# Moving one more shared chunk of a mixture-of-experts layer behind the last branch of a graph transformer kernel

## The chip, the cores and the metric

The kernel runs on one core of a Trainium2 chip. The metric is the device time of one execution in microseconds (us). The core has TensorE (PE, matmuls; its weight loads are shown apart as PEld), VectorE (DVE), ScalarE (ACT), GpSimd (POOL) and SyncE (SP), each with an instruction queue of its own that runs in order. Transfers are issued from SP (plain ones) and from POOL (indirect ones, with row numbers from a tile).

## The reference

The reference is a two-layer graph transformer over 3125 nodes with 256 features. Each layer adds a graph part, a mixing part and a feed-forward part to `x`. Only the feed-forward part of the second layer, a mixture of experts, is touched here:

```python
def _L1_ffn_ref(x, Wr, W1s, b1s, W2s, b2s, W1p, b1p, W2p, b2p):
    shared = gelu(x @ W1s + b1s) @ W2s + b2s          # every row; 256 -> 1024 -> 256
    rw = jax.nn.softmax(x @ Wr, axis=-1)              # 8 experts
    topw, topi = jax.lax.top_k(rw, K)                 # K = 2
    topw = topw / jnp.sum(topw, axis=-1, keepdims=True)
    mask = jnp.sum(jax.nn.one_hot(topi, E, dtype=topw.dtype) * topw[..., None], axis=-2)
    h = gelu(jnp.einsum('bsd,edf->bsef', x, W1p) + b1p)
    priv = jnp.einsum('bsef,efd->bsed', h, W2p) + b2p
    routed = jnp.einsum('bsed,bse->bsd', priv, mask)
    return shared + routed
```

Its input is the layer normalised `x`, and its result is added to `x`.

## The kernel before

The 3125 rows are 25 tiles of 125 rows. They are grouped in seven chunks (`CHUNKS`, line 23): chunks 0 to 5 hold four tiles (500 rows) and chunk 6 holds one (125 rows). The whole second layer is one function, `layer1`, with generators as its parts.

**The shared part** is `shared(c)` (line 1994). For a chunk it makes eight up groups (line 2012, tile `hp_s`: two matmuls each, `pw1s` against the turned rows `xT_f`), a gelu of each on ACT (line 2003, `hid_s`), and for each tile of 125 rows one down group of eight matmuls (line 2026, `dn_s`), whose result DVE adds to `X` (line 2029). A float32 matmul is recorded twice in the trace, so a chunk of 500 rows has 32 records on line 2012 and 64 on line 2026, 16 for each tile.

**The routed part** sorts the 6250 pairs of a row and an expert by expert. `scatter()` (lines 1975 to 1992) writes each row to its places in `xs` by 50 indirect transfers on POOL. The places are cut in `NT` = 32 tiles of 256 rows. `fetched(i)` (line 2032) fetches the expert's weights `rw` by two indirect transfers (line 2039), loads the rows `xr` on SP (line 2045) and turns them with PE (line 2056, `xrT`). The load waits for all 50 scatters. `routed(i)` (line 2065) is the two matmul layers with a gelu between them (line 2086, `rh`; line 2074; line 2101, `ry`), an addition of the bias on DVE (line 2108) and two indirect stores to `ys` on POOL (line 2111).

**The end.** `finish(t)` (line 2120) loads a tile's two routed results `yl` from `ys` (line 2123, two transfers each through `rows_dma`, line 208) and adds each with its gate to `X` on DVE (line 2126, two instructions a tile). The load comes after all stores (`stored_`). `collect(c)` (line 2130) stores a finished chunk to the output.

**The order of the work** is set by a planner, `Flow` (line 87), while the program is built. Each generator yields an `Op` with an engine, a cost in us, what it comes after, and buffers that it takes and gives back. `run` always issues the operation that can start earliest by these costs, and the lower urgency number where two start together. The engines then execute the instructions of each queue in that order. The buffers stand for real tiles: in this part PSUM has `mm` = 2, `nm` = 3 and `qe` = 2 banks (line 2223). `hp_s` takes `mm` and `qe` in turn, and both `ry` and `dn_s` take `nm`, which DVE's addition gives back. `shared` = 1 keeps two shared chunks from running at once. The eight `rhid` buffers hold the routed hidden rows and, at the end, the `yl` tiles.

The routed tiles that are always there and some of the shared chunks run in one long flow:

```python
            if c < LATE:
                flow.add(60 + c if c < 3 else 200 + c, shared(c))
...
            if i < NT - SPARE:
                flow.add(70 + i, routed(i))
```

The last `SPARE` = 2 routed tiles run in a branch, `tc.If(tiles > NT - SPARE)` (line 2181), which is taken only where the rows of the experts need more than 30 tiles. In the profiled execution it isn't taken (line 2086 has 960 records, 30 tiles of 32). Behind it a new flow with a clock of its own, the tail, holds the rest:

```python
        for c in range(LATE, len(CHUNKS)):
            shared_[c].time = None
        for c, (t0, nt) in enumerate(CHUNKS):
            if c >= LATE:
                flow.add(200 + c, shared(c))
            for t in range(t0, t0 + nt):
                flow.add(300 + c, finish(t))
            flow.add(300 + c, collect(c))
```

The costs that the planner has for the tail are: 0.0035 us a row for an up group (1.75 for 500 rows), 1.75 for four down matmuls, 0.42 for a shared addition, 0.6 with a lag of 3.5 for a `yl` load, 1.0 for a pair of routed additions, 0.1 for an output, and 0.2 between any two engines (`hop`). The planner takes all stores as done at time 0 of the tail.

Of the kernel before, what the change touches and what calls it, by code (L numbers as in the profile page):

```python
# [22 lines left out]
CHUNKS = [(t, min(4, T - t)) for t in range(0, T, 4)]  # L23
# [127 lines left out]
def kernel(ctx: ExitStack, tc: tile.TileContext, a: dict, out: bass.AP):  # L151
# [1311 lines left out]
    def layer1(lists):  # L1463
# [308 lines left out]


        RB = ROUTE // 128
        SPARE, LATE = 2, len(CHUNKS) - 2
        R = {"xT": [None] * len(CHUNKS)}
        logits_ = [Mark() for _ in CHUNKS]
        normal_ = [Mark() for _ in CHUNKS]
# [426 lines left out]
    def in_order():  # L2205
        with ExitStack() as st:
            psum(st, mm=4, nm=2, ed=2)
            first = Layer0(True)
            first.first()
            flow = Flow(mm=4, nm=2, ed=2, db=2, XT=5, qT=2, msg=2, S0=3, mlp=1, hT=1, hid=8,  # L2210
                        xh=2, xT=3, f_w=2, wT=1, ex=2, fh=3, qkv=2, q3=1)
            first.mixing_flow(flow)
            flow.add(-2, first.after_mixing())
            first.edges_flow(flow)
            first.mlp_flow(flow)
            flow.add(-2, first.after_mlp())
            first.soft_flow(flow)
            with tc.manual_schedule(engines=ENGINES):
                flow.run()
            for name in ("ffn", "fw", "e0"):  # L2220
                first.close(name)
        with ExitStack() as st:
            psum(st, mm=2, nm=3, qe=2, ed=1)
            layer1(True)

    def any_order():
# [40 lines left out]
        with ExitStack() as st:  # L2267
            psum(st, mm=2, nm=3, qe=2, ed=1)
            layer1(False)
# [104 lines left out]
```

## Time and profile before

| what | us |
|---|---|
| median of four runs | 2858.73 |
| lowest and highest of them | 2852.36, 2878.94 |
| the profiled execution | 2856.21 |
| its span in the trace | 2854.4 |
| PE busy in the span | 2513.8 (88%) |
| DVE, ACT, POOL busy | 1333.7, 975.3, 1180.6 |
| last scatter issued, first `xr` turned | 2339.98, 2355.59 |
| last routed matmul starts | within 2792.43 to 2796.05 |
| first `yl` load issued | 2807.07 |
| last addition starts | 2846.30 |

Times of the trace count from the start of its span. The page gives each engine's busy share in 40 slices, the chain of work that ended last, and the costliest groups of instructions by line. A row of a timeline has the start, the duration, the engine, the line, the operation with the names of its tiles, how many instructions are merged in the row, and in brackets how long the engine was idle before them and what ended that. A row of windows has a stretch, its length, the busy time of PE, PEld, DVE, ACT and POOL, the clock that TensorE was granted (1.00 is full), the DMA engines' share and GB/s.

### The profile page before, as it was taken

Reading aid. Unit: us, or ns where it says so; the run is one execution under the profiler, and the core shown is the slowest. Engines: PE = TensorE matmul, PEld = TensorE weight load, DVE = VectorE, ACT = ScalarE, POOL = GpSimd, SP = SyncE. Lnnn points to the kernel's source line nnn. Section 1 sums busy time; section 2 is a strip of 40 time slices with the busy share of each in tenths; the row PEclk is TensorE's granted clock in tenths of the full one; section 3 lists DMA queues with packets and bytes.
Section 4 is the critical chain, followed back from the end, with each engine's and each line's share of the span. In section 5 each row is a group of like instructions: output and inputs, shape, how many; then the busy total and the mean of one; then the engine's idle time right before and its main releaser. Section 6 shows DMA issues by size and latency. Waiting matters only on the chain. (4 is left out here: it accounts for less than half of the span.)

```text
span 2854.4 us, 31754 instructions
## 1 busy us (share of the span) xinstructions
PE 2513.8 (88%) x11281; PEld 1824.5 (64%) x11281; DVE 1333.7 (47%) x3223; ACT 975.3 (34%) x1997; POOL 1180.6 (41%) x1175
## 2 busy tenths in 40 slices
PE   3888898988899999996777888888888999999998
PEld 2545575655556555564555666666666768888886
DVE  5375113253343343445878687777788401111114
ACT  3673111221222333344334453444443212222221
POOL 3002676766674000002666566655562371222220
PEclk8989998999999999997889999989999999999999
DMA  4335556565564002506666556656550044555556
GB/s 107 127 103 168 156 152 187 156 172 170 153 201 111 26 15 75 130 22 209 209 189 202 172 186 195 180 161 193 183 173 31 19 133 149 194 194 194 194 194 192
DMA packets 186806, 426.48 MB, mean 149 GB/s; under 512 B 31370, under 2 KB 116490, under 8 KB 178443
## 3 DMA queue, kind: packets, MB, share of 16 engines
q0 software_dynamic: 80496, 281.25, 32.5%
q1 hardware_dynamic: 103593, 140.99, 15.8%
q10 hardware_dynamic: 2545, 2.09, 0.3%
q8 instruction: 92, 1.51, 0.2%
q14 instruction: 80, 0.65, 0.1%
HBM read 358.95 MB, written 65.22 MB: 149 GB/s over the span
## 5 line engine op out<-in xcount | busy, mean ns | idle before, releaser
L1083 POOL DMA_INDIRECT msg<-hs,el x425 | 418.0, 984 | 410.2 <-DMA hot<-S 210.5
L1524 POOL DMA_INDIRECT kvg<-kvtab,el x425 | 459.3, 1081 | 286.9 <-issue 116.7
L1195 ACT ACTIVATE fh<-fp,bnh,bns 128x500 f32<-128x500 f32 (+1 forms) x224 | 160.2, 723 | 406.8 <-PE fp L1191 291.6
L1601 PE MATMUL es<-kvg,S 128*125 128x264 f32 x850 | 226.9, 421 | 42.0 <-DVE kvg L1593 30.0
L1560 PE MATMUL qe<-q,ST 125*128 125x256 bf16 x1275 | 186.7, 291 | 65.1 <-DVE kvg L1564 41.9
L1206 DVE SCALAR_TENSOR_TENSOR x<-fy,f_w,x 125x256 f32<-125x256 f32 x200 | 95.8, 482 | 308.3 <-PE fy L1203 188.0
L1203 PE MATMUL fy<-f_Wo,fh 128*125 128x256 f32 x800 | 209.7, 386 | 29.5 <-DVE x L1206 17.3
L1601 PEld LDWEIGHTS es<-kvg,S 128*125 128x125 f32 x850 | 170.7, 206 | 89.9 <-DVE kvg L1593 39.3
L2086 PE MATMUL rh<-xrT,rw 128*128 128x256 f32 x960 | 223.7, 381 | 0.0
L2074 ACT ACTIVATE rhid<-rh,rw 128x256 f32<-128x256 f32 x240 | 113.7, 474 | 321.6 <-PE rh L2086 304.4
L1112 PEld LDWEIGHTS <-S 128*125 128x125 bf16 x1275 | 158.3, 142 | 96.3 <-issue 79.4
L2101 PE MATMUL ry<-rw,rhid 128*128 128x256 f32 x960 | 217.0, 379 | 0.0
L1112 PE MATMUL es<-msg,S 128*125 128x256 bf16 x1275 | 186.9, 283 | 27.6 <-DMA msg<-hs,el 14.7
L1560 PEld LDWEIGHTS <-ST 125*128 125x128 bf16 x1275 | 131.7, 103 | 110.5 <-issue 78.5
L2101 PEld LDWEIGHTS ry<-rw,rhid 128*128 128x128 f32 x960 | 182.4, 190 | 24.8
L1203 PEld LDWEIGHTS fy<-f_Wo,fh 128*125 128x125 f32 x800 | 142.8, 190 | 86.6 <-issue 33.4
L2086 PEld LDWEIGHTS rh<-xrT,rw 128*128 128x128 f32 x960 | 181.1, 191 | 24.1 <-issue 0.5
L1191 PE MATMUL fp<-fh,f_W 128*128 128x500 f32 (+1 forms) x448 | 187.8, 548 | 2.0 <-ACT fh L1195 2.0
L1191 PE MATMUL fp<-xT_f,f_W 128*128 128x500 f32 (+1 forms) x448 | 188.2, 548 | 0.0
L2108 DVE TENSOR_TENSOR yr<-ry,rw 128x256 f32<-128x256 f32 x60 | 25.5, 425 | 335.7 <-PE ry L2101 335.7
L1564 DVE TENSOR_TENSOR kvg<-qe,kvg 128x512 f32<-128x512 f32 (+1 forms) x225 | 144.6, 652 | 75.8 <-PE qe L1560 26.6
L1319 POOL TENSOR_TENSOR xn<-xn,row_bp 125x1024 f32<-125x1024 f32 (+1 forms) x7 | 13.8, 1975 | 386.7 <-DVE hx L1293 316.8
(426 smaller groups left out, 4246.2 us busy)
## 6 DMA issues: line engine op xcount, KB each, us to landing
db<-dlT SPq DMA_DIRECT2D x25, 544.0 KB
ST<-dlT SPq DMA_DIRECT2D x25, 544.0 KB
hot<-S SPq DMA_DIRECT2D x50, 187.5 KB
Sb<-hot SPq DMA_DIRECT2D x50, 187.5 KB
ztab<-z SPq DMA_DIRECT2D x18, 500.0 KB
z<-ztab SPq DMA_DIRECT2D x12, 750.0 KB
xs<-pad SPq DMA_DIRECT2D x1, 8224.0 KB
xr<-xs SPq DMA_DIRECT2D x32, 257.0 KB
```

The source lines that it names most:

```text
L1083: nc.gpsimd.indirect_dma_start(out=msg[:, i, :], out_offset=None, in_=hs3_rows, in_offset=bass.IndirectOffsetOnAxis(ap=el[:, b, g0 + i : g ...
L1112: nc.tensor.matmul(blk["po"], S[:, i, :], msg[:, i, r * C : (r + 1) * C], start=(g0 + i == 0 and r == 0), stop=(g0 + i == LE - 1 and r == 2))
L1191: nc.tensor.matmul(ps[q][:, :n], self.ws[e][i][:, k, q * 128 : (q + 1) * 128], h[:, k, :n], start=(k == 0), stop=(k == 1))
L1195: nc.scalar.activation(nxt[:, q, :n], ps[q][:, :n], AF.Relu, bias=self.sh[i][:, 2 * e + q : 2 * e + q + 1], scale=self.sc[i][:, 2 * e + q ...
L1203: nc.tensor.matmul(po, nxt[:, k, j * P : (j + 1) * P], self.ws[e][2][:, k, :], start=(k == 0), stop=(k == 1))
L1524: nc.gpsimd.indirect_dma_start(out=kvg[:, i, : 2 * C], out_offset=None, in_=kvtab, in_offset=bass.IndirectOffsetOnAxis(ap=el[:, b, g0 + i ...
L1560: nc.tensor.matmul(pq[i0][:, i, :], ST[:P, g0 + i0 + i, :], blk["q3"][:, r, :], start=(r == 0), stop=(r == 2))
L1564: nc.vector.tensor_tensor(kvg[:, i0 : i0 + k, :C], pq[i0][:, :k, :], kvg[:, i0 : i0 + k, :C], OP.mult)
L1601: nc.tensor.matmul(blk["pa"], S[:, i, :], kvg[:, i, C:], start=(g0 + i == 0), stop=(g0 + i == LE - 1))
L2074: nc.scalar.activation(hid[-1][:, q % 2, :], ps, AF.Gelu, bias=w1[:, 8 * C + q : 8 * C + q + 1])
L2086: nc.tensor.matmul(ps, w1[:, k * 4 * C + h * 128 : k * 4 * C + (h + 1) * 128], xrT[:, k, :], start=(k == 0), stop=(k == 1))
L2101: nc.tensor.matmul(po, hid[k // 2][:, k % 2, r * 128 : (r + 1) * 128], w2[:, k * C : (k + 1) * C], start=(k == 0), stop=(k == 7))
```

## The change

`LATE` is the number of the first shared chunk that runs in the tail. It was 5 and becomes 4.

```diff
         RB = ROUTE // 128
-        SPARE, LATE = 2, len(CHUNKS) - 2
+        SPARE, LATE = 2, len(CHUNKS) - 3
         R = {"xT": [None] * len(CHUNKS)}
```

`shared(4)` (32 records of line 2012, 8 gelus, 64 records of line 2026, 4 additions) is no longer a stream of the long flow. It becomes a stream of the tail, with the same urgency 204, ahead of `shared(5)` (205) and `shared(6)` (206). The tail then has three shared chunks, 500, 500 and 125 rows, beside the 25 loads and 25 pairs of additions. Nothing is computed that wasn't before, and no transfer is added or left out.

## The prediction

> **What bounds the kernel now.** I read the stage table of the page first: over the whole span PE is busy 88%, and from 2250 us on it shows 100% in nearly every slice. So I asked for the windows around the routed stage and the tail, in rows cut where the work changes.
>
> ```profile
> 2341.80:2352.00 10.20, 10.20 (x25) 4.37 (x23) 0.42 (x1) 3.39 (x5) 3.52 (x4) 1.00 0.88 310
> 2352.00:2355.50 3.50, 0.02 (x1) 0.00 (x0) 0.02 (x1) 0.00 (x0) 0.00 (x0) 0.79 1.01 415
> 2355.50:2364.00 8.50, 6.35 (x18) 4.78 (x19) 1.60 (x4) 1.52 (x3) 0.00 (x0) 0.50 0.38 120
> 2364.00:2796.00 432.00, 432.00 (x2053) 379.02 (x2052) 47.70 (x118) 113.71 (x240) 115.44 (x117) 1.00 0.54 188
> 2807.00:2820.50 13.50, 13.50 (x33) 6.16 (x34) 8.03 (x17) 4.74 (x7) 0.00 (x0) 1.00 0.90 206
> 2834.30:2841.50 7.20, 7.18 (x49) 6.38 (x47) 5.33 (x13) 2.94 (x8) 0.00 (x0) 1.00 0.90 269
> 2841.50:2854.40 12.90, 0.00 (x0) 0.00 (x0) 2.73 (x7) 0.00 (x0) 0.00 (x0) 0.66 0.44 125
> ```
>
> After the window and its length stand the busy us of PE, PEld, DVE, ACT and POOL, then the granted clock, DMA share and GB/s. The reader is to see three things: PE is the bound from 2364 to 2841.5 without a gap; just ahead of that it waits, at clock 0.50 when it resumes; and in the tail from 2807 the DMA (0.90) is as busy as PE, and the last 12.9 us hold no PE work.
>
> Then PE's timeline, to find where chunk 4 (16 up and 32 down matmuls, recorded as 32 and 64) runs today:
>
> ```profile
> 2341.80 10.22 PE L2012 MATMUL hp_s<-xT_f,pw1s 128*128 128x500 f32 x24
> 2355.59 1.09 PE L2056 MATMUL xrT<-ident,xr 128*128 128x128 f32 x4 [3.57 <-DMA xr<-xs]
> 2363.03 2.47 PE L2012 MATMUL hp_s<-xT_f,pw1s 128*128 128x500 f32 x4
> 2381.74 1.84 PE L2012 MATMUL hp_s<-xT_f,pw1s 128*128 128x500 f32 x4
> 2398.98 1.89 PE L2026 MATMUL dn_s<-pw2s,hid_s 128*125 128x256 f32 x8
> ...
> ```
>
> ```profile
> 2790.70 1.89 PE L2026 MATMUL dn_s<-pw2s,hid_s 128*125 128x256 f32 x8
> 2792.43 3.62 PE L2101 MATMUL ry<-rw,rhid 128*128 128x256 f32 x16
> 2795.88 1.89 PE L2026 MATMUL dn_s<-pw2s,hid_s 128*125 128x256 f32 x8
> 2797.61 0.60 PE L2056 MATMUL xrT<-ident,xr 128*128 128x128 f32 x4
> 2798.04 8.80 PE L2026 MATMUL dn_s<-pw2s,hid_s 128*125 128x256 f32 x40
> 2806.99 13.65 PE L2012 MATMUL hp_s<-xT_f,pw1s 128*128 128x500 f32 x32
> ```
>
> Chunk 4 stands in two places where it is free. 24 up records (10.2 us) lie in the wait for the scattered rows, which ends with the DMA at 2355.5 whatever PE does. 48 down records (10.4 us) lie behind the last routed matmul (end 2796.05), beside the last two stores. Only 24 records stand in the PE-bound stretch.
>
> Last DVE's timeline of the tail, for its order:
>
> ```profile
> 2824.94 1.00 DVE L2126 SCALAR_TENSOR_TENSOR x<-yl,gate,x 125x256 f32<-125x256 f32 x2 [1.37 <-DMA yl<-ys]
> 2826.24 1.00 DVE L2126 SCALAR_TENSOR_TENSOR x<-yl,gate,x 125x256 f32<-125x256 f32 x2 [0.30 <-DMA yl<-ys]
> 2827.42 1.01 DVE L2126 SCALAR_TENSOR_TENSOR x<-yl,gate,x 125x256 f32<-125x256 f32 x2 [0.17 <-DMA yl<-ys]
> 2828.34 0.42 DVE L2029 TENSOR_TENSOR x<-dn_s,x 125x256 f32<-125x256 f32 x1
> ```
>
> Chunk 5's first down tile leaves PE at 2823.9 (2820.48 + 3.45), but its addition runs at 2828.34, behind fourteen pairs of routed additions (28 instructions of L2126 from 2810.57), which wait for transfers.
>
> **The change part by part.** No instruction or byte is added: chunk 4 leaves the long flow and becomes the first shared chunk of the tail.
>
> *The scatter wait.* The 24 up records leave the cover. PE idles from 2341.8 to 2355.6 instead of 3.5 us; xr lands when it did. The clock was already at 0.50 on resuming, so the ramp is unchanged. Cost here 0; the 10.2 us reappear in the tail.
>
> *The routed stage.* Four pieces leave it: 2.31 (2363.03 to 2365.34), 1.68, 1.72 and 1.73 us (starts to the next start), 7.44 in all; 0.63 of the first is slow clock (its 4 records take 1.68 warm), which falls on routed matmuls instead. So 6.81 earlier: the last routed matmul ends at 2796.05 - 6.81 = 2789.24. Bounds: 1.73 if the three early pieces covered waits that open again, 7.44 if all of it is won. I take 6.81, since nothing is idle from 2364 to 2796.
>
> *The stores and loads.* From the last routed matmul to the first yl load is 11.0 us today (weights issue 2796.78, two stores at 2798.05 and 3.59 us landing after 2803.34, load at 2807.07). POOL's chain doesn't hold chunk 4, so the loads start 6.81 earlier, at 2800.26. SP keeps its order of loads and outputs; only chunk 4's output now waits for its addition, behind all loads.
>
> *PE in the tail.* PE need not wait for the stores. After the last transposes (0.43) and the branch (0.15 of gap today) chunk 4 starts at 2789.8; its up part takes 13.49 (2806.99 to 2820.48), ending at 2803.3; three down tiles at 3.45 end at 2813.7. The fourth needs a PSUM bank: tag nm has three, and the first returns with chunk 4's first addition on DVE.
>
> *DVE's order, the new wait.* The planner restarts its clock at 0 for the tail. By its costs the loads are ready from 0.6 + 3.5 + 0.2 = 4.3, one addition pair per 1.0; the first shared addition is ready at 14.0 + 3.5 + 0.2 = 17.7. So fourteen pairs stand ahead of it, then three between neighbours: exactly the order in the trace, and chunk 4 now takes chunk 5's place. But the plan starts PE and loads together (they did: 2806.99 and 2807.07), and now PE starts 10.4 before the loads. The first addition comes, as today, 2828.76 - 2807.07 = 21.69 us after the loads' start: 2821.95. PE stands idle from 2813.7 to 2821.95, 8.3 us, and chunk 5's up matmuls are queued behind on PE, then ACT's gelus behind those. Behind DVE's waiting pairs only shared additions are queued. The other banks return in time (second addition 2833.63 - 6.81 = 2826.8).
>
> *The clock after that stall.* After 5.63 us of idle at 588.47 the clock was 0.50 until about 592.6, a loss of 2.1; after 3.57 and 2.06 at 2355.5 it cost 3.2 (6.35 busy at half). I take 2.2, nearer the single gap; ends 2.1 and 3.2, and not less, since both rows lost it. The Trainium skill's page "TensorE: Matmul & The Clock Gate" (Part 1, What's actually happening) speaks against such a gap: one idle window of about 3.4 us halves the clock and a busy window of 3.4 us restores it. By that alone the loss would be an estimated 1.7, and the total 0.5 lower than mine.
>
> *Sum.* Fourth tile 3.45 + 2.2 from 2822.0: 2827.65. Chunks 5 and 6 as today, 34.49 (2806.99 to 2841.48): 2862.14. Last addition 0.05 later; from its start to the end of the span 8.1 today (2846.30 to 2854.4): 2870.3. Against 2854.4 that is +15.9. The profiled execution took 2856.21 (1.81 around its span): 2872.1. The median of the runs, 2858.73, lies 2.5 above the profiled time; I keep to the profiled one.
>
> **The rivals.**
>
> No stall: the additions come in time, if DVE's order were other than I worked out. Then PE runs through: 2789.8 + 27.30 (13.49 up, 13.81 down) + 34.49 = 2851.6, end 2859.7, time 2861.5 (+5.3). For it: PE has no gap in the tail today. Against: today's margin was 2.1 us (fourth tile due at 2830.9, bank back at 2828.76), and PE moves 10.4 ahead.
>
> All loads first: the planner puts chunk 4's additions behind all 25 pairs. The first addition would come 39.2 + 0.4 after 2800.26, at 2839.9; + 5.65 + 34.49 + 8.1 ends at 2888.1, time 2890. Against: the order read in the trace and the same costs in the planner.
>
> Faster: today chunk 4's half-done down tile holds one nm bank from 2398.98 to 2790.70, so routed tiles have two. With three, some 27 tiles could shrink; it decides from 15.9/27 = 0.6 us a tile on; at 1.0 the time is 2845. Against: a tile's 64 records at 0.2157 and 0.43 of transposes make 14.24, and that is its period (2683.16 to 2697.41). There is nothing to win.
>
> PE held at the branch until the stores land: start 2800.2, no bank stall, 61.8 of work and about 2.2 of clock: 2864.3, end 2872.4, time 2874. Against: ACT passes the branch at 2788, when its own work ends. It hardly differs from the forecast.
>
> **How the numbers follow.** Stall 0.72, no stall 0.13, held at the branch 0.06, all loads first 0.06, faster 0.03. The prediction is the stall's, 2872. Its own ends: routed pieces won less (up to +5.1), clock +1.0, the 2.5 between profile and median: 2870 to 2881. The range takes in the no-stall case at 2861.5 less the clock and output tail's small change: 2859 to 2882. One per cent, about what a measurement of this kernel can tell from no change, is 28.6: slower than 2887.3 is all loads first and little else, 0.07; faster than 2830.1 needs 1.6 us a tile, 0.01; within, 0.92.
>
> **What would show it.** Right: PE idle about 13.8 us before 2355.6; yl loads starting near 2800; a PE gap of about 8 us inside L2026 in the tail that ends with DVE's L2029, the clock 0.5 after it; PE's end about 20 us after today's. Wrong: L2026 of the tail without a gap, a shared addition that DVE runs before the fourteenth pair, or a routed period other than 14.25.

## The result and the profile after

The changed kernel takes 2874.29 us (median) beside 2859.91 for the kernel before, a ratio of 1.0049 with a 95% interval of 1.0038 to 1.0060. That is slower by 14.4 us. It lies inside the one per cent that the prediction took for no change, and the interval tells it from no change all the same. Its profiled span is 2867.6 us against 2854.4.

These are the rows of windows of the changed kernel, cut as before where the stages allow it.

```profile
2341.80:2352.00 10.20, 0.00 (x0) 0.00 (x0) 0.00 (x0) 0.00 (x0) 2.59 (x3) 0.57 0.95 341
...
2364.00:2780.00 416.00, 416.00 (x1987) 366.29 (x1986) 46.83 (x116) 111.36 (x236) 113.19 (x115) 1.00 0.55 191
...
2813.00:2822.00 9.00, 1.99 (x5) 1.61 (x6) 6.02 (x14) 0.00 (x0) 0.00 (x0) 0.75 0.89 264
2822.00:2826.00 4.00, 4.00 (x14) 3.17 (x13) 3.35 (x8) 0.00 (x0) 0.00 (x0) 0.70 0.93 257
...
2830.00:2862.00 32.00, 30.14 (x135) 22.48 (x133) 6.85 (x16) 7.01 (x15) 0.00 (x0) 1.00 0.25 69
```

The wait for the scatter (first row) now holds no PE work at all, where it held 10.20 us. The routed stage is full as before. New are the hole in PE at 2813 to 2822, the lower clock behind it, and a last stretch in which PE works while the DMA engines are nearly empty (0.25, where the tail before had 0.90).

PE's timeline of the changed kernel shows the same as instructions:

```profile
2354.84 1.11 PE L2056 MATMUL xrT<-ident,xr 128*128 128x128 f32 x4 [14.06 <-DMA xr<-xs]
...
2788.93 13.65 PE L2012 MATMUL hp_s<-xT_f,pw1s 128*128 128x500 f32 x32 [0.15 <-PEq L2181]
2802.42 10.52 PE L2026 MATMUL dn_s<-pw2s,hid_s 128*125 128x256 f32 x48
2820.01 5.88 PE L2026 MATMUL dn_s<-pw2s,hid_s 128*125 128x256 f32 x16 [7.07 <-DVE x L2029]
2825.72 13.58 PE L2012 MATMUL hp_s<-xT_f,pw1s 128*128 128x500 f32 x32
...
```

Three of chunk 4's four down tiles run at once (48 records); the fourth waits 7.07 us, and the bracket names DVE's shared addition on line 2029 as what ended it. It then takes 5.88 us, where a warm tile's row has 3.62.

DVE's timeline of the changed kernel around that addition, and SP's first load:

```profile
2816.30 2.04 DVE L2126 SCALAR_TENSOR_TENSOR x<-yl,gate,x 125x256 f32<-125x256 f32 x4 [1.32 <-DMA yl<-ys]
2818.61 1.01 DVE L2126 SCALAR_TENSOR_TENSOR x<-yl,gate,x 125x256 f32<-125x256 f32 x2 [0.28 <-DMA yl<-ys]
2819.53 0.42 DVE L2029 TENSOR_TENSOR x<-dn_s,x 125x256 f32<-125x256 f32 x1
```

```profile
2798.36 11.95 SPq L208 DMA_DIRECT2D yl<-ys  x22
```

Fourteen pairs of L2126 (28 instructions from 2802.50 on) precede the addition at 2819.53, although PE had its operand ready at about 2805.9 (2802.42 and 3.45 for a tile). Nothing that the trace shows kept DVE from it but its place in the queue; the second run below tests this.

**How the traces are compared.** The stages ahead of the scatter are not touched, yet they move by up to 19 us between executions on one chip (the last scatter is issued at 2335.19 to 2354.17). A second and a third chip, on which the later runs were made, are quicker there by some 144 us: the kernel before takes 2704 and 2707 us on them. Each ratio below is against the kernel before on the same chip. Stages are counted from the issue of the last scatter:

| us from the last scatter | last routed matmul ends | loads start | PE ends | span ends |
|---|---|---|---|---|
| before | 456.1 | 467.1 | 501.5 | 514.4 |
| before, third chip | 454.9 | 465.8 | 500.3 | 510.7 |
| changed | 449.6 | 459.6 | 521.4 | 528.9 |
| changed, second chip | 449.3 | 459.7 | 520.9 | 528.3 |

The changed kernel's stages repeat within 0.6 us over two chips. The kernel before, whose end hangs on loads, repeats over two chips within 1.3 up to PE's end and within 3.7 at its end. So from single traces differences of 1 to 2 us can be read up to PE's end, but only those above some 4 at the end of the span. PE's end is 19.9 later with the change (20.6 between the repeats), and the span's end 14.4 (17.5), because the kernel before ends 10 to 13 us behind PE and the changed one 7.4.

### The profile page after: what moved, and what is told of

Same layout as the page of the kernel before. It is cut to its first block, busy times and chain, and to the rows that moved or that the text cites. A ratio compares the mean times of both kernels' runs of the same rounds, so it can differ in the third digit from the quotient of the medians.

```text
span 2867.6 us, 31753 instructions
## 1 busy us (share of the span) xinstructions
PE 2515.6 (88%) x11281; PEld 1823.1 (64%) x11281; DVE 1338.2 (47%) x3223; ACT 975.2 (34%) x1997; POOL 1176.7 (41%) x1175
## 5 line engine op out<-in xcount | busy, mean ns | idle before, releaser
L1560 PE MATMUL qe<-q,ST 125*128 125x256 bf16 x1275 | 181.2, 285 | 65.2 <-DVE kvg L1564 38.2
L1203 PE MATMUL fy<-f_Wo,fh 128*125 128x256 f32 x800 | 211.5, 388 | 21.7 <-DVE x L1206 11.1
L1319 POOL TENSOR_TENSOR xn<-xn,row_bp 125x1024 f32<-125x1024 f32 (+1 forms) x7 | 13.8, 1975 | 387.3 <-DVE hx L1293 317.3
```

Source lines behind the costliest of these rows:

```text
L1203: nc.tensor.matmul(po, nxt[:, k, j * P : (j + 1) * P], self.ws[e][2][:, k, :], start=(k == 0), stop=(k == 1))
L1560: nc.tensor.matmul(pq[i0][:, i, :], ST[:P, g0 + i0 + i, :], blk["q3"][:, r, :], start=(r == 0), stop=(r == 2))
```

## The experiments

**A fourth bank.** The theory was that the gap is a PSUM bank held by an addition that stands late in DVE's queue. The rivals were that the gap costs nothing, or that PE waits for something else. Edit of the changed kernel:

```diff
+                    bank = "ed" if c == LATE and j == 3 else "nm"
-                    m = yield Op("PE", 1.75, [acts[q + 3]], take=["nm"] if q == 0 else [],
+                    m = yield Op("PE", 1.75, [acts[q + 3]], take=[bank] if q == 0 else [],
...
-                        po = nm_tile([P, C], f"dn_s{c}_{j}")
+                        po = ps_tile(bank, [P, C], f"dn_s{c}_{j}")
...
-                m = yield Op("DVE", 0.42, [m], give=["nm"])
+                m = yield Op("DVE", 0.42, [m], give=[bank])
...
```

Beyond these lines, the planner's buffers get `ed=1` beside `nm=3`.

> The changed kernel, but the fourth down tile of chunk 4 writes to the idle PSUM bank of tag ed, so it waits for no addition; DVE's order is the same. Theory (the bank held by DVE's late additions): the gap of 7.07 and the slow restart of 2.26 go, 9.3 in all: PE ends near 2850.8 in the trace's time, 2865 us against 2874 changed and 2860 before, ratio to before 1.0018. Rival one (chunk 4 costs only what it lost of its cover, and the gap is hidden by the loads, which set the end): no change, ratio 1.0049. Rival two (PE waits in the tail for the transfers or the branch, not for a bank): the gap stays, ratio 1.0049.

Measured: ratio 1.0018 (0.9998 to 1.0039), median 2864.28. PE's timeline of this kernel:

```profile
2785.00 13.65 PE L2012 MATMUL hp_s<-xT_f,pw1s 128*128 128x500 f32 x32
2798.49 13.98 PE L2027 MATMUL dn_s<-pw2s,hid_s 128*125 128x256 f32 x64
2812.30 13.58 PE L2012 MATMUL hp_s<-xT_f,pw1s 128*128 128x500 f32 x32
...
```

All four down tiles run as one row of 64 (line 2027 here, by the edit), and chunk 5 follows at once. DVE's order is unchanged: the first shared addition still stands behind fourteen pairs of routed ones (28 instructions from 2798.33 on), and by then PE is at chunk 5:

```profile
2815.87 0.42 DVE L2030 TENSOR_TENSOR x<-dn_s,x 125x256 f32<-125x256 f32 x1
```

PE ends 511.5 after the last scatter, 9.9 earlier than in the changed kernel, and the span ends 518.8, 10.1 earlier. Both rivals fall: the gap was a bank, and it was paid.

**DVE's order.** If the bank is late because of the order, then a better order should do what a bank does. Edit of the changed kernel:

```diff
+        for m in stored_:
+            m.time = 9.4
         for c in range(LATE, len(CHUNKS)):
             shared_[c].time = None
```

> The changed kernel, but the planner takes the stores as done at 9.4 instead of 0 of the tail, about what the traces show between PE's first shared matmul and the first load. DVE's first shared addition then stands behind 4 routed pairs instead of 14; banks and work are the same. Theory (DVE's order is what holds the bank): the same 9.3 are won as with a fourth bank, ratio to before 1.0018. Rival (it isn't the order, but too few banks for any order): the gap stays, 1.0049.

Measured: ratio 1.0028 (1.0005 to 1.0050), median 2866.88; PE ends 510.3 after the last scatter, the span 517.7. DVE's timeline of this kernel:

```profile
2813.83 1.01 DVE L2126 SCALAR_TENSOR_TENSOR x<-yl,gate,x 125x256 f32<-125x256 f32 x2 [0.50 <-DMA yl<-ys]
2814.75 0.42 DVE L2029 TENSOR_TENSOR x<-dn_s,x 125x256 f32<-125x256 f32 x1
2815.09 3.92 DVE L2126 SCALAR_TENSOR_TENSOR x<-yl,gate,x 125x256 f32<-125x256 f32 x8
...
```

The addition now stands behind four pairs, PE has no gap, and three banks are enough. The rival falls. The interval of the ratio holds the theory's 1.0018 and the rival's 1.0049 alike; the trace carries this verdict.

**The down half alone.** This tells the lost cover from the stall: the up half stays in the long flow. Edit of the changed kernel (`shared` cut in two, `shared_up` and `shared_down`):

```diff
             if c < LATE:
                 flow.add(60 + c if c < 3 else 200 + c, shared(c))
+            elif c == LATE:
+                flow.add(200 + c, shared_up(c, True))
...
-                flow.add(200 + c, shared(c))
+                flow.add(200 + c, shared_down(c, True) if c == LATE else shared(c))
```

(with `LATE` at 4, as in the changed kernel)

> Only the down half of chunk 4 moves to the tail; its up half stays in the wait for the scatter, so no cover is lost. The planner's order puts 3, 3 and 4 pairs between chunk 4's additions, then 15 pairs ahead of chunk 5's first. Theory: chunk 4 no longer stalls, but the fourth down tile of chunk 5 needs the bank of its first one, which comes only after all 25 pairs, some 39 us after the loads start: a gap of about 11 there, 2868 against 2860, ratio 1.003. Rival (the lost cover is the whole loss of the change): PE ends as before, the loads start 3.5 earlier, ratio 0.999.

Measured: ratio 1.0019 (0.9998 to 1.0039), median 2868.5; the span ends 521.8 after the last scatter. PE's timeline of this kernel:

```profile
2826.49 10.52 PE L2043 MATMUL dn_s<-pw2s,hid_s 128*125 128x256 f32 x48
2847.99 6.15 PE L2043 MATMUL dn_s<-pw2s,hid_s 128*125 128x256 f32 x16 [10.98 <-DVE x L2046]
...
```

The lines stand lower by the edit (2043 for the down matmuls, 2046 for the shared addition). The stall moved to chunk 5, as worked out from the order, with a gap of 10.98 where about 11 was expected, and DVE runs the three additions of chunk 5 that had waited only at 2847.52, behind all 25 pairs. So the stall belongs to no chunk: it comes wherever the fourth down tile meets an addition that the planner put behind loads. The rival falls by the trace: PE ends 514.4 after the last scatter, 12.9 later than in the kernel before, where the rival had no difference. The interval of the ratio lies above the rival's 0.999 too, but by less than 0.001.

**The down half alone, with the better order.** The two edits together.

> The down half alone in the tail, and the planner's stores at 9.4. Theory: no cover lost and no bank stall. PE's end is that of before (2841.5), the loads start 3.5 to 4 earlier, since two pieces of 1.72 leave the routed stage: 2856.5 against 2860, ratio 0.9988. Rival (the tail is bound by DVE's additions or by the outputs whatever the order): 1.000 or more.

Measured first: ratio 1.0004 (0.9981 to 1.0027), which leaves it open. It was run once more on the third chip.

> The down half alone in the tail with the planner's stores at 9.4, once more, since its first interval (0.9981 to 1.0027) left open whether it beats the kernel before. By its trace (512.4 against 514.4 from the last scatter) the ratio is 0.9993; a rival that the trace missed a cost would show as 1.001 or more.

Measured there: ratio 0.9983 (0.9970 to 0.9997), medians 2702.37 and 2706.85. PE's last rows on that chip:

```profile
2668.63 13.98 PE L2043 MATMUL dn_s<-pw2s,hid_s 128*125 128x256 f32 x64
...
2686.01 3.62 PE L2043 MATMUL dn_s<-pw2s,hid_s 128*125 128x256 f32 x16
```

Chunk 5's four down tiles run without a gap. PE ends 502.2 (first chip) and 501.1 after the last scatter, within 1 us of the kernel before (501.5 and 500.3). So with cover kept and stall gone all but 1 us of the 20 at PE's end is gone. The span ends 512.4 and 510.8, which is 2.0 earlier and 0.1 later than before; both are below what single traces tell. The small gain of the second measurement is thus not traced to a place.

**Four chunks in the tail.** The lost cover, made larger: `LATE = len(CHUNKS) - 4`.

> Four shared chunks in the tail instead of three (chunk 3 too). Chunk 3 ran wholly in the wait for the scatter, so all of its 27.4 us of PE work loses its cover; its additions stand behind 14 routed pairs just as chunk 4's do in the changed kernel. Theory (each piece taken out of that wait is paid in full, and the bank stall is paid once): PE's end comes 27.4 later than in the changed kernel, 548.8 after the last scatter against 521.4; about 2902 us, ratio to before 1.0145; one gap of 7 in the tail. Rival (the tail's loss is the stall alone, and more chunks fit beside the loads): ratio 1.005. Rival (a stall for each chunk of 500 rows): a second gap and 2910 or more.

Measured: ratio 1.0171 (1.0155 to 1.0187), medians 2749.76 and 2703.65. PE ends 549.2 after the last scatter (548.8 expected). PE's timeline of this kernel:

```profile
2657.93 10.52 PE L2026 MATMUL dn_s<-pw2s,hid_s 128*125 128x256 f32 x48
2676.94 6.36 PE L2026 MATMUL dn_s<-pw2s,hid_s 128*125 128x256 f32 x16 [8.49 <-DVE x L2029]
...
2696.55 13.98 PE L2026 MATMUL dn_s<-pw2s,hid_s 128*125 128x256 f32 x64
...
2723.78 13.98 PE L2026 MATMUL dn_s<-pw2s,hid_s 128*125 128x256 f32 x64
...
```

There is one gap for three chunks of 500 rows, and what is taken out of the scatter's wait is paid in full: PE idles 40.47 us there where the changed kernel on this chip idles 13.19, 27.3 more. That PE's end came so near the expected 548.8 is in part luck. Beside the repeat of the changed kernel on the same chip it is 28.4 later: 27.2 are chunk 3's work, the stall and its slow restart are 2.2 longer (8.49 and 6.36 beside 6.71 and 5.96), and the routed stage ends 1.0 earlier. The expected ratio was too small: it was reckoned against the first chip's longer time and later end. The end of the span is 46.3 later than in the repeat of the kernel before (557.0 against 510.7), and 0.0171 of 2703.65 is 46.2.

**One chunk in the tail.** The change the other way: `LATE = len(CHUNKS) - 1`.

> The change the other way: only chunk 6 stays in the tail, chunk 5 joins the long flow. In the planner's order chunks 4 and 5 are then finished before the last two routed tiles, so the last routed matmul ends 37 later than before (10.4 of chunk 4 that lay behind it, and 27.3 of chunk 5), and the loads start that much later with almost no PE work beside them. Theory (a shared chunk is worth having in the tail as long as the loads are the longer side): loads start 504 after the last scatter, end 552, 2896 us, ratio 1.013. Rival (PE work is only reordered, so the total stays): 1.000 to 1.002.

Measured: ratio 1.0102 (1.0082 to 1.0122), medians 2727.63 and 2703.65. Slower as expected, but not in the expected way. The last routed matmul ends 456.2 after the last scatter, as before: the reading of the planner's order was wrong, and chunk 5 lies behind that matmul. Yet the loads start at 494.3, 38.2 after that matmul, where it is 11.0 in the kernel before. PE's end is 501.6, as before, so the loss lies in the loads and additions behind it: the span ends at 540.6 (552 expected). SP's waits in this kernel (engine and line, what it waited for, us in all, times, longest):

```profile
SPq L208 <- DMA ys<-yr,to: 36.3, 1, 36.3
SPq L208 <- PEq L2181: 28.5, 1, 28.5
...
```

Behind the wait for the stores SP waits another 28.5 us for PE's queue at line 2181, the branch. PE gets there only when chunk 5, which it has ahead of the branch, is done. So here the last event ahead of the loads is PE's passing of the branch (2679.2, the first load at 2679.30). By these waits the loads start at the later of two events: the last store has landed, and PE has passed the branch.

**Earlier stores in the kernel before.** In the kernel before the two events coincide (PE passes at 2806.9, the load is issued at 2807.07), so either could have held the loads. This run moves one of them. Edit: a generator of its own issues a routed tile's first store when its own half is added.

> The kernel before with one edit: a routed tile's first store is issued when its own half is added; chunk 4 stays where it was. The last two stores then land about 4.5 earlier. Theory (from the run with one chunk in the tail: the first load waits for PE to pass the branch too, and PE still has 10.4 of chunk 4 ahead of the branch): the loads still start 10.9 to 11 after the last routed matmul, nothing is gained, ratio 1.000. Rival (the loads wait for the stores alone): they start 6.6 after it, the end comes 4 earlier, ratio 0.9985.

Measured: ratio 0.9992 (0.9979 to 1.0004). The loads start 10.95 after the last routed matmul, no earlier than before. SP's waits:

```profile
SPq L208 <- DMA ys<-yr,to: 33.9, 1, 33.9
...
SPq L208 <- PEq L2190: 3.7, 1, 3.7
...
```

The stores are done 3.7 us sooner and nothing is won: in the kernel before, too, chunk 4's 10.4 us of PE work ahead of the branch hold the loads.

**Earlier stores, with the down half alone and the better order.** Here PE passes the branch right after the last routed tile.

> The down half alone in the tail with the planner's stores at 9.4, and besides a routed tile's first store is issued when its own half is added, not after both; the same transfers. The last tile's two stores then don't follow each other, and the loads start about 6.6 after the last routed matmul instead of 11.5. Theory (with the stall gone the tail's end is set by loads and additions, 10 us behind PE's end): the end comes 3 earlier than without it, held then by PE: 509.5 after the last scatter, against 512.4 without it and 514.4 before; ratio to before 0.998. Rival (the loads are slowed by the last weights that are fetched beside them, or a later weight fetch delays the routed tiles): no gain or a loss, 1.000 or more.

Measured: ratio 0.9987 (0.9975 to 0.9999), medians 2701.22 and 2703.65. The loads start 9.1 after the last routed matmul instead of 11.2 to 11.5 without the edit, so less was won there than the 5 expected (from the last store's issue to the first load it is 7.1, where it is 2.9 in the same kernel without this edit and 3.7 in the kernel before; that the last weights, fetched just ahead of it, slow it was not tried); the span ends 510.1 after the last scatter (509.5 expected), and PE at 501.2. By its ratio it beats the kernel before by about a tenth of a per cent (the interval ends just below 1), and with it the changed kernel; it isn't told apart from the same kernel without the earlier stores (0.9983).

**Repeats.** Both kernels once more, the changed one on the second chip and the one before on the third; their stages are in the table above, their times 2724.68 and 2709.42.

> The changed kernel once more, for how far the stages of one execution repeat: if the times counted from the last scatter repeat within about 1 us while the time of the last scatter itself moves by several, differences of 2 us in the routed stage and the tail can be read from single traces. Expected from the last scatter: loads 459.6, PE's end 521.4, end of the span 528.9.

> The kernel before once more, for how far its stages repeat. Expected from the last scatter: last routed matmul ends 456.1, loads 467.1, PE's end 501.5, end of the span 514.4.

## Why the prediction was right

The forecast was +15.9 us of span. The traces give +13.2 between the profiled spans, +14.4 and +17.5 from the last scatter, and the medians +14.4 (0.49%). The mechanism held: the lost cover, the bank held by DVE's order and the slow restart are each in the traces, and two runs take the stall away, one by a fourth bank and one by DVE's order. The absolute time, 2872 against 2874.29, is nearer than the sum deserves. It starts from a profiled execution of 2856.21 where the median before is 2859.91, and the rise that it adds is 1.5 too large; the two errors partly cancel.

- *The scatter wait.* 13.8 us of idle PE were expected and 14.06 came; the granted clock was 0.50 on resuming in both kernels, and the 10.2 us reappeared at PE's end. The run with four chunks shows the same for chunk 3's 27 us.
- *The routed stage.* 6.81 earlier was expected; 6.5 and 5.5 came. The period stayed 14.25, so the rival with a bank more won nothing.
- *The stores and loads.* This is the step that was mis-sized. The prediction kept 11.0 us from the last routed matmul to the first load and put all of it down to POOL's chain. It is 10.0 and 10.4 in the changed kernel. The 11.0 before was held by PE at the branch as well, which two runs showed later. So the second place of chunk 4 that the prediction called free, the 10.4 us behind the last routed matmul, was not quite free (about 0.8 us, estimated from the last store's issue to the first load: 3.73 before, 2.91 with the change). The prediction asked whether PE waits for the stores at the branch (it doesn't: 2788.93 against loads at 2798.36) and not whether the loads wait for PE.
- *DVE's order and the bank.* Fourteen pairs, and 21.6 us from the first load to the end of the first shared addition against 21.69. The gap is 7.07 instead of 8.3, mostly since the loads came about 1 sooner after the last routed matmul.
- *The clock.* 2.26 lost (5.88 against 3.62) where 2.2 was taken. The other stalls lost 2.3 to 2.7 (5.96, 6.15 and 6.36). In windows of 0.1 us the granted clock stays at 0.50 for 4.4, 4.6, 5.0 and 5.4 us after PE's return (the changed kernel, its repeat, the down half alone, four chunks), and half of each is about what was lost. The Trainium skill's page "TensorE: Matmul & The Clock Gate" (Part 1, What's actually happening) would have had an estimated 1.7: its rule names the right effect, but its 3.4 us of slow clock, counted from the first matmul, is shorter than any of the four. The traces also show why the loss varies: from its fall to its rise the clock was low for 6.83, 6.83, 13.65 and 10.24 us, which is 2, 2, 4 and 3 times 3.41, and it rose at the end of the first such step that PE was busy from end to end. So the loss depends on where in a step PE comes back (an estimate from these steps: half of one to two of them, 1.7 to 3.4 us), and that 2.2 came so near 2.26 is luck.
- *The end.* From the start of the last addition to the end of the span 7.4 instead of 8.1.

Of the 19.9 us at PE's end, the cover takes about 10.5 (idle of 14.06 against 3.57), the bank 7.07 and the restart 2.26. The fourth bank took 9.9 of them away, the better order 11.1, and keeping the up half where it was, with the better order, all but 0.7 (502.2 against 501.5).

## What to carry to other kernels

Work that fills a wait is free only there: before it is moved, ask what fills the hole that it leaves, since its time comes back wherever it goes. A planner that restarts its clock assumes that all engines start together; where one gets ahead, the other's in-order queue puts ready work behind waits, and a few shared banks then stop the first engine too. And behind a branch, work that an engine still has ahead of it can hold another engine's transfers.

## What the runs showed of the hardware

A load behind a branch that isn't taken also waited for PE to pass that branch: 28.5 us beyond the stores with one chunk in the tail, 3.7 with earlier stores. That it waits because its `yl` tiles reuse the `rhid` buffers, which the branch's matmuls read, is read from the code; no run tried other buffers. The engines passed the branch each on its own: in the changed kernel ACT at 2782.0, when its own work ended, PE at 2788.8 and POOL at 2796.1.

In the four traces with a stall the granted clock stayed at 0.50 for whole steps of 3.41 us. In the changed kernel it fell at 2817.59, 4.6 us after PE's last matmul, and rose at 2824.42, two steps later; in the other three it was low for 2, 4 and 3 steps.

Three chips ran the same kernel before in 2860, 2704 and 2707 us; from the last scatter to PE's end the first and the third differ by 1.2 of 501, and nearly all the rest lies in the stages ahead of it. Why two of them are quicker there wasn't tried.
